# Reordering the turns of two 16-head attentions: a projection between first and second scores, the products behind them in the projection's bank, and VectorE's spare work bound behind the addition of maxima

## The chip, the cores and the metric

The kernel runs on one NeuronCore of a Trainium2 chip, as one program. The metric is the device time of one execution in microseconds (us). A NeuronCore has five engines that take their own instructions in the order in which the program lists them and wait for one another through semaphores: TensorE (PE; its weight loads are listed as PEld), VectorE (DVE), ScalarE (ACT), GpSimd (POOL) and SyncE (SP, which here only issues DMAs). Matrix products go to PSUM, which is cut into banks; SBUF is the on-chip memory, HBM the main one.

## The reference, cut to what matters

The model is a decoder of two layers on 8 batches of 256 tokens of 256 channels, all in float32. Each layer is a mixer, a cross attention and a last block, with a residual sum and a layer norm behind each:

```python
x = layernorm(x + L0_attn(x))    # a gated convolution
x = layernorm(x + L0_xattn(x))   # cross attention with 77 keys
x = layernorm(x + L0_ffn(x))     # shared and routed experts
x = layernorm(x + L1_attn(x))    # 16-head self attention with rotary embedding
x = layernorm(x + L1_xattn(x))   # cross attention
x = layernorm(x + L1_ffn(x))     # 16-head self attention with split masks
```

Only the fourth and the sixth matter here. Both project x to queries, keys and values of 16 heads of 16 channels and compute `softmax(q k^T * scale) v`, then an output projection and a bias. The fourth (called the first attention below) turns queries and keys by the rotary tables. The sixth (the second attention) splits the tokens into "positive" and "negative" ones by a similarity to a guide vector; each token attends only to its own class and to five register tokens, and the register tokens take the mean of both classes.

## The kernel before

The program runs the six blocks one after another; blocks overlap a little at their seams. Everything that the change touches is in the class `Heads16`, which both attentions use (`Rotary` for the first, `split` for the second), and in the list of extra work that `split` hands to it.

**A turn.** An attention has 8 batches, and a batch 4 groups of 4 heads, so `Heads16.run` makes 32 turns and two more to empty the pipeline. In turn i the loop issues:

- `scores(i)` (matmuls L1032): first scores, queries by keys, into two double banks of the pool tag `sc`. VectorE then takes the negated row maxima with two reductions (L1038).
- `products(i - 2)` (L1080): probabilities by values, into the single bank `op`. ScalarE copies the result to `o` (L1087), and in all batches but the last SP copies the rows with the sums of the softmax out into a compact tile `comp` (L1093).
- `exponentials(i - 1)` (L1061): second scores, keys by shifted queries, so that they come out transposed and with the maximum subtracted, into two more double banks of `sc`; ScalarE takes two exponentials from them into `pT` (L1069).
- the extra work of place 0: TensorE work in the bank `op`, such as transposes of finished tokens (L89), the register tokens' scores (L1535), the transposes of their probabilities (L1559) and their products (L1569).
- the extra work of place 1: a projection of a later batch (L1005 queries and keys, L1014 values) or the output projection of an earlier one (L1127), in the single bank `mm`, which ScalarE or VectorE empties.
- `turn_maxima(i)` (L1048): two transposes of the maxima into `op`; VectorE adds them to the queries, which gives the shifted queries `qs` (L1207 in the first attention, L1434 in the second).
- the extra work of place 2, mostly VectorE's: the reciprocals of the sums (L1100; SP writes them back as `rows`, L1102), the spreading and application of them (`wide` L1111, `o` L1119, `oT` L1122), the rotation of a later batch's queries and keys (`sw` L1226, then GpSimd L1230 to L1237), the statistics of a finished batch's layer norm (L111, L112), which GpSimd completes (L114, L115, L117), and the register tokens' softmax (L1546, L1553, then GpSimd L1554).

The `sc` pool has three double banks and a turn takes four, in rotation. So the second half of the second scores goes into the bank that the first half of the same turn's first scores had, and it has to wait for the first reduction.

**Whose order counts.** The framework puts instructions on each engine's queue by its own estimate of when they can run; `tc.issue_after(x)` holds everything issued inside it behind x on x's own engine. `bound(f)` holds TensorE's instructions of f behind TensorE's newest one, so TensorE's order is that of the code. All other work of a turn is held behind the turn's second reduction on VectorE, and what follows the second scores also behind the last exponential on ScalarE.

**The extra work by turns.** For batch b and t = 4b the first attention lists: the projections of queries and keys of batch b+1 in turns t+1 and t, their rotation one turn later, its values in t+3, the reciprocals in t+4 and t+6, `normed` (L1111 to L1122) in t+5 and t+7, the output projection in t+10 (t+8 for the last two batches), the layer norm (`finish`) in the turn after that, and the transposes of the finished tokens (`turn_out`, L89) in the second turn after it. The second attention lists the register tokens' four steps in t, t+1, t+2 and t+3, the same reciprocals, `normed`, output and `finish`, and the projections of batches 5 to 7, in turns given by hand in `at_turn`; batches 0 to 4 are projected ahead of the loop.

## Time and profile before

| | |
|---|---|
| median of 3 runs | 1399.26 us (1399.0 to 1399.41) |
| the profiled execution | 1399.1 us, of which its span on the core is 1397.3 us |
| busy share of the span | PE 96%, PEld 66%, DVE 57%, ACT 36%, POOL 30% |
| first attention | its turn 0 starts at 710.35 us, turn 31 at 888.32 us |
| second attention | its turn 0 starts at 1188.30 us, turn 31 at 1362.95 us; the span ends at 1397.3 us |

A page of the profile gives shares of the whole span, but the change touches two stretches of it, so those have to be read by themselves. The timeline lists start, length, engine, line, operation and tiles of each instruction or run of like ones, and in square brackets how long the engine sat idle before it and who ended that. "Granted clock" (PEclk) is the share of TensorE's full speed in a stretch.

The length of a turn is read from one first-score matmul to the next. In the middle of the first attention four turns take 6.06, 5.66, 5.67 and 5.67 us (turns 20 to 23 start at 827.18, 833.24, 838.91 and 844.57 us, turn 24 at 850.24); in the middle of the second, 5.13, 5.66, 5.84 and 6.56 us (turns 16 to 19 start at 1278.96, 1284.10, 1289.76 and 1295.60 us, turn 20 at 1302.16).

### The profile page before, as it was taken

Reading aid. Unit: us, or ns where it says so; the run is one execution under the profiler, and the core shown is the slowest. Engines: PE = TensorE matmul, PEld = TensorE weight load, DVE = VectorE, ACT = ScalarE, POOL = GpSimd, SP = SyncE. Lnnn points to the kernel's source line nnn. Section 1 sums busy time; section 2 is a strip of 40 time slices with the busy share of each in tenths; the row PEclk is TensorE's granted clock in tenths of the full one; section 3 lists DMA queues with packets and bytes.
Section 4 is the critical chain, followed back from the end, with each engine's and each line's share of the span. In section 5 each row is a group of like instructions: output and inputs, shape, how many; then the busy total and the mean of one; then the engine's idle time right before and its main releaser. Section 6 shows DMA issues by size and latency. Waiting matters only on the chain.

```text
span 1397.3 us, 21759 instructions
## 1 busy us (share of the span) xinstructions
PE 1335.6 (96%) x8521; PEld 928.5 (66%) x8521; DVE 793.6 (57%) x1514; ACT 496.5 (36%) x738; POOL 420.7 (30%) x467
## 2 busy tenths in 40 slices
PE   8999999999999999999989999899999998899994
PEld 3554578888876666656566666577878887566652
DVE  3776555565643423323656777755556662677774
ACT  3455532333331123221215444343332323344441
POOL 0100012223200123326423757332343545123322
PEclk9999999999999999999999999999999999899997
DMA  9000043334340012332130000025232210000000
GB/s 284 2 1 0 0 149 111 85 96 154 125 196 0 23 57 87 88 124 83 30 106 3 4 2 3 2 84 165 79 98 61 62 37 2 24 9 29 16 19 23
DMA packets 79113, 88.16 MB, mean 63 GB/s; under 512 B 13476, under 2 KB 73796, under 8 KB 78500
## 3 DMA queue, kind: packets, MB, share of 16 engines
q1 hardware_dynamic: 75604, 77.46, 17.7%
q0 software_dynamic: 3408, 9.31, 2.4%
q8 instruction: 68, 1.11, 0.3%
q14 instruction: 33, 0.27, 0.1%
HBM read 56.77 MB, written 29.52 MB: 62 GB/s over the span
## 4 chain that ended last, share of the span: by engine, by line
PE 71%; DVE 6%; POOL 3%; issue 2%; DMA 2%; SPq 0%; ACT 0%; POOLq 0%; DVEq 0%; ACTq 0%
PE mm L521 9%; PE sc L476 8%; PE mm L778 7%; PE ps_sc L1061 6%; PE ps_sc L1032 5%; PE mm L841 5%; PE op L1080 4%; PE tr L795 4%; PE ps_mm L1005 2%; PE tr L855 2%; PE ps_mm L1127 2%; PE sc L505 2%; PE sc L375 2%; PE sc L411 2%; PE sc L457 1%
## 5 line engine op out<-in xcount | busy, mean ns | idle before, releaser
L1038 DVE TENSOR_REDUCE mx<-ps_sc 128x4 f32<-128x1024 f32 x128 | 150.9, 1221 | 41.0 <-PE ps_sc L1032 40.9
L521 PE MATMUL mm<-Ub,pT 128*128 128x256 f32 (+1 forms) x640 | 144.6, 379 | 0.5 <-ACT pT L75 0.4
L496 POOL TENSOR_TENSOR p<-p,sm 128x616 f32<-128x616 f32 x60 | 72.7, 1216 | 240.1 <-DVE sm L493 213.5
L1069 ACT ACTIVATE pT<-ps_sc 128x1024 f32<-128x1024 f32 x128 | 124.1, 1021 | 56.6 <-PE ps_sc L1061 56.6
L476 PE MATMUL sc<-M,xT_s 128*128 128x308 f32 x512 | 139.0, 423 | 1.1 <-ACT pT L75 1.1
L521 PEld LDWEIGHTS mm<-Ub,pT 128*128 128x128 f32 (+1 forms) x640 | 120.8, 190 | 20.0 <-ACT pT L75 0.9
L476 PEld LDWEIGHTS sc<-M,xT_s 128*128 128x128 f32 x512 | 94.4, 188 | 35.3 <-ACT pT L75 2.1
L778 PE MATMUL mm<-xT_s,w 128*128 128x512 f32 x256 | 113.4, 595 | 2.1 <-DVE h L784 2.1
L489 ACT ACTIVATE p<-p 128x616 f32<-128x616 f32 x64 | 45.9, 716 | 154.6 <-DVE p L485 132.8
L1061 PE MATMUL ps_sc<-qs,kp 32*128 32x256 f32 x1024 | 99.4, 417 | 0.9 <-DVE mx L1038 0.9
L1061 PEld LDWEIGHTS ps_sc<-qs,kp 32*128 32x128 f32 x1024 | 64.9, 192 | 35.9 <-issue 26.6
L778 PEld LDWEIGHTS mm<-xT_s,w 128*128 128x128 f32 x256 | 47.8, 190 | 56.0 <-issue 52.6
L815 POOL DMA_INDIRECT xb<-xd,token x39 | 37.1, 952 | 146.4 <-PE tr L822 81.2
L483 DVE TENSOR_REDUCE nmx<-sc 128x8 f32<-128x616 f32 x64 | 51.1, 799 | 46.4 <-PE sc L476 46.3
L1080 PE MATMUL op<-pT,va 128*32 128x256 f32 x1024 | 71.3, 398 | 4.6 <-DVE qs L1207 4.0
L841 PE MATMUL mm<-wE,xbT 128*128 x156 | 73.5, 593 | 0.3 <-ACT xbT L827 0.3
L1087 ACT COPY o<-op 128x256 f32<-128x256 f32 x64 | 23.8, 373 | 131.8 <-PE op L1080 131.8
L492 DVE TENSOR_REDUCE sm<-p 128x8 f32<-128x616 f32 x64 | 50.6, 790 | 22.2 <-ACT p L489 21.8
L114 POOL TENSOR_SCALAR rstd<-mv 128x2 f32<-128x2 f32 x48 | 12.3, 255 | 166.9 <-DVE mv L112 166.8
L117 DVE TENSOR_SCALAR x_s<-r,mv,rstd 128x256 f32<-128x256 f32 x66 | 26.0, 436 | 60.9 <-POOL rstd L115 60.9
L827 DVE COPY hT<-tr 128x256 f32<-128x256 f32 x39 | 16.6, 425 | 75.7 <-PE tr L822 75.7
L181 PE MATMUL pair<-xT_s,w 128*128 128x512 f32 x128 | 58.3, 615 | 0.9 <-DMA w<-in_W_inT 0.9
(307 smaller groups left out, 2490.4 us busy)
## 6 DMA issues: line engine op xcount, KB each, us to landing
Ub<-ud SPq DMA_DIRECT2D x32, 512.0 KB
ud<-U SPq DMA_DIRECT2D x16, 616.0 KB
wE<-in_wE SPq DMA_DIRECT2D x4, 1536.0 KB
yd<-y SPq DMA_DIRECT2D x39, 128.0 KB
Ub<-ud SPq DMA_DIRECT2D x32, 104.0 KB
ud<-U SPq DMA_DIRECT2D x4, 608.0 KB
x_s<-in_x SPq DMA_DIRECT2D x8, 256.0 KB
w<-in_Wo SPq DMA_DIRECT2D x2, 1024.0 KB
```

Of the source, the lines that this page charges most:

```text
L181: last = nc.tensor.matmul(ps[:, i, :], w_in[:, kc, c * P : (c + 1) * P], xT_s[:, kc, :], start=kc == 0, stop=kc == 1,)
L476: nc.tensor.matmul(sc[:, a, : 4 * NCTX], xT_b[:, kc, j * P : (j + 1) * P], M[:, a * 4 : a * 4 + 4, kc, at : at + NCTX], start=kc == 0, sto ...
L496: engine.tensor_tensor(pv, pv, bcast(sm, 2, [P, 8, NCTX]), ALU.mult)
L521: nc.tensor.matmul(o[:, j * D : (j + 1) * D], pT[:n, c, j * P : (j + 1) * P],  Us[b][:n, g, c], start=g == 0 and j == 0 and c == 0, stop=g ...
L778: nc.tensor.matmul(ps, w[:, kc, cols], xT_s[:, kc, :], start=kc == 0, stop=kc == 1)
L795: nc.tensor.matmul(o[:, j * D : (j + 1) * D], hs[c][:, at : at + P], w3[:, c, :], start=c == 0, stop=c == 7,)
L841: nc.tensor.matmul(ps, xT[:, kc, :], column(j, kc * 512, 512), start=kc == 0, stop=kc == 1)
L1032: nc.tensor.matmul(scs[s // 2][:, s % 2, qb * SEQ : (qb + 1) * SEQ], self.queries(b, c, s, m)[:, qb * P : (qb + 1) * P], self.keys(b, c, s ...
L1038: self.last = nc.vector.tensor_reduce(self.mx[m][:, :, 2 * j : 2 * j + 2, self.free[m]].rearrange("p q s -> p s q"), scs[j].rearrange("p s ...
L1061: nc.tensor.matmul(scs[s // 2][:, s % 2, kb * SEQ : (kb + 1) * SEQ], self.keys(b, c, s, m)[:, kb * P : (kb + 1) * P], qs[s * 32 : (s + 1) ...
L1069: last = nc.scalar.activation(pT[:, 2 * j : 2 * j + 2].rearrange("p s k t -> p s (k t)"), scs[j], AF.Exp)
L1080: nc.tensor.matmul(ps[s * 32 : (s + 1) * 32, :SEQ], va[:, kb, 8 * c + 2 * s + m, :], pT[:, s, kb, :], start=kb == 0, stop=kb == 1, tile_po ...
```

## The change

Within a turn the order on TensorE becomes: first scores, place 0, place 1, second scores, products, transposes of the maxima. This holds where a turn has work of place 1 as well as products and second scores; then the products' copy on ScalarE stands between the two exponentials. In a turn without work of place 1 the products stay ahead of the second scores, but place 0 is still moved ahead of both. The products go to the bank `mm` in place of `op`. Work of place 2 is held behind `shifted`, the addition that makes `qs`, on VectorE. In the second attention the projections move to other turns, and `fill(0)` in the part ahead of the loop stands two steps later in the code.

```diff
-        def exponentials(self, i):
+        def exponentials(self, i, between):
...
-            for j in range(2):
-                last = nc.scalar.activation(
+            def exp(j):
+                return nc.scalar.activation(
                     pT[:, 2 * j : 2 * j + 2].rearrange("p s k t -> p s (k t)"), scs[j], AF.Exp
                 )
-            return last
+
+            first = exp(0)
+            with tc.issue_after(first.ins), tc.issue_after(self.newest(PE)):
+                copied = between()
+            with tc.issue_after((copied or first).ins):
+                return exp(1)
...
-            va, pT, ps = self.vals[b % 2], self.pT.pop(i), self.side()
+            va, pT, ps = self.vals[b % 2], self.pT.pop(i), self.mm()
...
                 with tc.issue_after(self.last.ins), ExitStack() as st:
-                    if 0 <= i - 2 < n:
+                    for f in work.pop((i, 0), ()):
+                        bound(f, self.side())
+                    other, products = work.pop((i, 1), ()), 0 <= i - 2 < n
+                    for f, end in other:
+                        ps = self.mm()
+                        bound(f, ps)
+                        end(ps)
+                    late = products and other and i - 1 < n
+                    if products and not late:
                         bound(self.products, i - 2)
                     if 0 <= i - 1 < n:
-                        st.enter_context(tc.issue_after(bound(self.exponentials, i - 1).ins))
-                    for f in work.pop((i, 0), ()):
-                        bound(f, self.side())
-                    ends = []
-                    for f, end in work.pop((i, 1), ()):
-                        ps = self.mm()
-                        bound(f, ps)
-                        ends.append(lambda end=end, ps=ps: end(ps))
+                        bound(
+                            self.exponentials, i - 1,
+                            lambda: self.products(i - 2) if late else None,
+                        )
                     if i < n:
-                        bound(self.turn_maxima, i)
-                    for f in ends + work.pop((i, 2), []):
+                        st.enter_context(tc.issue_after(bound(self.turn_maxima, i).ins))
+                    for f in work.pop((i, 2), []):
                         f()
...
-            at_turn = ((5, 9, 13), (11, 15, 17), (19, 21, 23))
+            at_turn = ((7, 8, 11), (12, 15, 16), (19, 20, 23))
...
             for i in range(3):
                 early(0, i)
-            fill(0)
             turn_last(at.mm())
             early(1, 0)
             add_last(at.mm())
+            fill(0)
```

`turn_maxima` and both `shifted` now return the addition's instruction, and `products` its copy, so that the loop can hold other work behind them.

More of the change, by code (lines that the diff above doesn't have):

```diff
@@ L948, in experts @@
         ]
+    PE = mybir.EngineType.PE
     class Heads16:
@@ L1052, in turn_maxima @@
             qs = self.qs[i] = self.c2.tile([P, SEQ], F32, tag="qs", name="qs")
-            self.shifted(b, c, m, qs, ps[:, :SEQ])
-        def exponentials(self, i):
+            return self.shifted(b, c, m, qs, ps[:, :SEQ])
+        def exponentials(self, i, between):
             b, k = divmod(i, 4)
@@ L1086, in products @@
             o = self.o[b, c]
-            nc.scalar.copy(o[:, m], ps[:, :SEQ])
+            copied = nc.scalar.copy(o[:, m], ps[:, :SEQ])
             if b == NB - 1:
-                return
+                return copied
             if m == 0:
@@ L1096, in products @@
             )
+            return copied
         def inverted(self, b, c):
@@ L1144, in run @@
             n = 4 * NB
-            pe = mybir.EngineType.PE
             def bound(f, *args):
-                with tc.issue_after(self.newest(pe)):
+                with tc.issue_after(self.newest(PE)):
                     return f(*args)
@@ L1206, in shifted @@
         def shifted(self, b, c, m, dst, maxima):
-            nc.vector.scalar_tensor_tensor(
+            return nc.vector.scalar_tensor_tensor(
                 dst, self.qrs[b % 2][:, c, :], self.cs["meets"][:, m : m + 1], maxima,
@@ L1433, in shifted @@
             def shifted(b, c, m, dst, maxima):
-                nc.vector.tensor_tensor(dst, qms[b][:, m, c, :], maxima, ALU.add)
+                return nc.vector.tensor_tensor(dst, qms[b][:, m, c, :], maxima, ALU.add)
             at = Heads16(st, queries, keys, shifted)
```

## The prediction

> **What bounds the kernel now.** I read the page's busy times, then its chain, then the two attentions alone by stretches and by timeline, since a share of the whole span averages six blocks.

> ```profile
> PE 1335.6 (96%) x8521; PEld 928.5 (66%) x8521; DVE 793.6 (57%) x1514; ACT 496.5 (36%) x738; POOL 420.7 (30%) x467
> ...
> PE 71%; DVE 6%; POOL 3%; issue 2%; DMA 2%; SPq 0%; ACT 0%; POOLq 0%; DVEq 0%; ACTq 0%
> ```

> The first line is busy time, the second the chain that ended last. TensorE sets the time nearly alone, so a change can win only where TensorE is busy without need, and loses wherever TensorE is made to wait. Busy by stretch (start:end, length, PE, PEld, DVE, ACT, POOL, PEclk, DMA share, GB/s), for turns 16 to 19 of the first attention and for its end:

> ```profile
> 804.10:827.20 23.10, 23.10 (x240) 15.95 (x239) 17.20 (x32) 11.04 (x16) 14.66 (x16) 1.00 0.02 3
> 892.10:905.00 12.90, 8.86 (x64) 5.37 (x65) 7.03 (x20) 3.94 (x6) 3.98 (x5) 0.74 0.01 1
> ```

> In a steady turn TensorE never stops; behind a stop of 4.04 us (892.41 to 896.45) its granted clock is halved for 6.83 us. Turns 19 and 20, by timeline:

> ```profile
> 821.51 1.15 PE L1032 MATMUL ps_sc<-kp,qr 32*128 32x256 f32 x16
> ...
> 822.63 1.07 PE L1080 MATMUL op<-pT,va 128*32 128x256 f32 x16
> 822.69 2.36 DVE L1038 TENSOR_REDUCE mx<-ps_sc 128x4 f32<-128x1024 f32 x2 [0.21 <-PE ps_sc L1032]
> ...
> 823.63 1.48 PE L1061 MATMUL ps_sc<-qs,kp 32*128 32x256 f32 x16
> ...
> 824.97 0.75 DVE L111 BATCH_NORM_STATS2 st<-r 128x6 f32<-128x256 f32 x2
> 825.04 1.99 PE L1014 MATMUL ps_mm<-w,xT_s 128*128 128x256 f32 x8
> ...
> 826.32 0.30 POOL L114 TENSOR_SCALAR rstd<-mv 128x2 f32<-128x2 f32 x1 [0.59 <-DVE mv L112]
> ...
> 826.70 0.89 POOL L115 TENSOR_TENSOR rstd<-rstd,nhalf 128x2 f32<-128x2 f32 x1
> 826.87 0.38 PE L1048 MATMUL op<-ident,mx 128*128 128x128 f32 x2
> ...
> 827.29 0.48 DVE L1207 SCALAR_TENSOR_TENSOR qs<-qr,cst,op 128x256 f32<-128x256 f32 x1 [0.27 <-PE op L1048]
> 827.70 2.43 POOL L117 TENSOR_SCALAR x_s<-r,mv,rstd 128x256 f32<-128x256 f32 x2
> ...
> 830.71 0.66 PE L89 MATMUL op<-ident,x_s 128*128 128x128 f32 x4
> ```

> Two things to see. The second scores take 1.48 where they take 1.09 in turns in which the first reduction is done already: 0.36 us of every turn is a wait, the gain that is to be had. And the layer norm of a batch starts at 824.97, 1.90 ahead of the maxima's transposes (T, 826.87), and ends at 830.13, 5.16 later; L89 reads it at 830.71. The margin is 0.58 us. In the second attention the register tokens' probabilities have the same shape:

> ```profile
> 1288.22 0.16 DVE L1553 RECIPROCAL nsm<-nsm 128x1 f32<-128x1 f32 x1
> ...
> 1288.48 0.66 POOL L1554 TENSOR_SCALAR nsl<-nsl,nsm 128x256 f32<-128x256 f32 x1 [1.75 <-DVE nsm L1553]
> ...
> 1289.45 0.38 PE L1048 MATMUL op<-ident,mx 128*128 128x128 f32 x2
> ...
> 1293.29 0.44 PE L1559 MATMUL op<-ident,nsl 128*128 128x128 f32 x2
> ```

> They are ready 0.31 before T and are read 3.8 after it.

> **The change, part by part.** All times are counted from T, the start of a turn's L1048.

> *1. Projection ahead of the second scores.* A turn is then first scores 1.08, projection 1.83, second scores 1.09, products 1.00, T 0.34: 5.34. The projection hides the 0.36. One more change of matmul shape costs an unknown amount: nothing at best; the step from first scores to products, with a change, shows 0.1 at most, so bounds 0 to 0.2; I take 0.1. So 5.43 against 5.67, **-0.24**, in 12 turns of the first attention: -2.9. Turns 1 to 5, where the projections are many, give -1.6 by the same sum (0.36 less, where it is there).

> *2. Place 2 bound behind qs.* Now this work starts 0.45 + 0.48 = 0.93 after T instead of before T, so it stands ahead of the next turn's two reductions (2.36). `wide`, `o`, `sw`, `oT` take 1.72 together. So the reductions end at 0.93 + 1.72 + 2.36 = 5.0. In turns 10, 14, ... 30 the output projection is then emptied by VectorE's sum with `xb` (0.69), which stands behind the reductions: 5.7. The products now need that bank (part 4): with 0.15 of handing over, 1.0 of products, T comes at 6.85 instead of 5.67: **+1.2** in 6 turns, +7.2. Bounds: +0.2 (if only the second scores waited) to +1.4. Turn 6, which has no projection to cover, goes from 4.02 to about 4.97: +0.95. Reciprocals with or without `sw` (0.24, 0.91) fit in the 5.43.

> *3. Place 0 moved to right behind the first scores.* This is the dear one. The layer norm (L111) now starts at T + 0.93 - 0.1, and takes 5.16 plus 0.35 for the `va` copies (0.74, ahead of rstd on POOL by the changed order, half of it beside VectorE's part): done at T + 6.3. TensorE reaches L89 at T + 0.34 + 1.08 = T + 1.4. **It waits 4.9** (bounds 4.4, with the first half of x_s 1.22 earlier and little else late, and 5.2). Behind it in TensorE's queue stand the projection, the second scores, the products and T; ScalarE's exponentials and VectorE's qs wait for these. Turns 12, 16, 20, 24: 6.3 + 0.4 (rest of L89) + 1.92 + 1.09 + 1.0 = 10.7 against 6.06, +4.7 each, +18.8. Turn 28, which had 5.33, has 8.9: +3.6. At the end, L89 of the sixth batch, behind turn 31, stands in the same way: +3 (0 to 5).

> Sum of the first attention: -1.6 - 2.9 + 7.2 + 0.95 + 18.8 + 3.6 + 3 = **+29.0**.

> *The second attention.* Here place 0 has the transposes L1559 behind POOL's `nsl`. Its chain starts behind qs: T + 0.87, and 1.58 from `wide` to `nsl` (1287.56 to 1289.14): ready at T + 2.4, asked for at T + 1.4: **+1.0** in 8 turns, those of remainder 2. The projections moved by `at_turn` go from turns of remainder 1 (5.67, then 3.98) into those of remainder 0 (5.13, then 6.73, since 2.65 of VectorE's work stands ahead of the reductions); remainder 3 goes from 6.56 to 6.37. By groups: turns 1 to 5 -3.6, 6 and 7 +0.6, 8 to 11 +0.1, 12 to 23 +1.9, 24 to 27 0, 28 to 30 +1.2. The `rows` DMAs stand behind the outputs and `kp` loads on SP's queue; a spreading that waits for them now holds back the reductions too: up to 6, I take +2.9; tail +1. Sum **+4.1** (-4 to +12).

> *4. Products in the bank `mm`, and ScalarE's copy between the exponentials.* The projection's copy (0.59) has the second scores' 1.09 to hide in; the products' copy (0.37) has the first scores' 1.08. The second exponential comes 1.4 later, and is next needed by products a turn on, 4 us away. Nothing, except where VectorE empties the bank (part 2). The move of `fill(0)` changes no order on VectorE or POOL: nothing; ±1 bounds it.

> *5. The clock.* Five waits (turns 12 to 28) are longer than any steady one. Stops of 2.15 and 2.19 (676.6, 160.6) leave PEclk at 1.00; one of 2.38 (714.65) and one of 4.04 halve it for 6.83. A wait of 3.7 for the first half of x_s and 0.9 for the second should halve it. Behind it L89 takes 0.91 against 0.49, a projection 2.5 against 1.83, second scores 2.02 against 1.09: +2.0 each, **+10** (0 to 17).

> [...]

> **Sum.** 1399.1 + 29.0 + 4.1 + 10 = 1442.2. The profiled execution (span 1397.3 and 1.8 around it) is 0.16 below the median of 1399.26. I say **1442**.

> **Rivals.**

> *The clock holds.* Two stops here left it at 1.00. Then 1432. Against it: 4.04 and 2.38 did not.

> *VectorE becomes the bound.* Everything late on VectorE delays its reductions, these T, and T the place 2 work; if SP's rows (6 instead of 2.9) and the clock (17) take their upper ends, and split +5 more, 1442 + 3 + 7 + 5 = 1457. For it: VectorE has 17.20 of 23.10 already. Against it: in most turns TensorE's own 5.43 is longer.

> *On the other side: place 2 leaves the path.* If VectorE ran this work in idle time ahead of T (it has 5.9 idle of 23.10), the reductions would start as now, so part 2 costs nothing; and if x_s were complete by T + 1.4, thus the layer norm 4.9 earlier, L89 would not wait and the clock would not fall. Then parts 1 and 3 leave -1.6 - 2.9 in the first attention and, with `nsl` 1.0 earlier, -4 in the second: **1391**. It decides on where L111 comes to run: it pays from 4.9 earlier on, and at today's 1.9 ahead of T (3.26 after T done) would still wait 1.9. The changed order has L111 behind qs, which speaks against it.

> *It does nothing on balance:* the wait of 0.36 stays, because another operand of the second scores is late, and part 3 is hidden by something I overlook: 1399.

> **How the numbers follow.** The forecast, 1442 with its bounds 1432 to 1452: 0.68. Clock holds, 1432 and a little below: 0.12. VectorE, 1457: 0.12. Covered waits, 1391: 0.05. Nothing: 0.03. The range must leave out at most 2 in 10: it runs from the low ends (clock 0, split -4 and stalls 4.4: 1442.2 - 10 - 8 - 2.5, about 1422, less 2 for the +0.2 of part 2 in some turns: 1420) to the third case, 1458. A measurement of this kernel can tell 0.2%, 2.8 us, from no change. Faster 0.05, same 0.03, slower 0.92.

> **What would show it.** Turns of the first attention by their first scores: 10.7, 5.4, 6.8, 5.4 in place of 6.06, 5.66, 5.67, 5.67; at their head L89 idle 3.7 and 0.9 behind POOL's x_s, and PEclk at half behind it; second scores at 1.09 in late turns (part 1); products idle behind VectorE's r in turns 10 to 30 (part 2); L1559's successor in the second attention idle 1.0 behind `nsl`. If L89 starts without a wait, or turns of remainder 0 take under 7 us, the prediction is wrong at its largest term.

## The result and the profile after

The changed kernel takes **1443.76 us** (median of 4 runs, 1443.15 to 1444.23) against 1399.13 us (4 runs, 1398.86 to 1399.41): a ratio of **1.0319**, with a 95% interval of 1.0301 to 1.0337. The profiled execution has a span of 1442.4 us, 45.1 more than before. The forecast was 1442, with a range of 1420 to 1458.

Busy time by engine, and the chain that ended last, on the page of the changed kernel:

```profile
PE 1352.7 (94%) x8521; PEld 928.5 (64%) x8521; DVE 786.9 (55%) x1514; ACT 495.4 (34%) x738; POOL 420.5 (29%) x467
...
PE 66%; DVE 8%; POOL 5%; issue 3%; DMA 2%; ACT 1%; SPq 1%; POOLq 0%; DVEq 0%; ACTq 0%
```

Lines are numbered by each run's own kernel: L1032, L1048, L1061, L1080, L1207 and L1559 of the kernel before are L1034, L1050, L1064, L1088, L1219 and L1571 here.

The same 8521 matmul records take 17 us longer, though none was added: the mean granted clock fell from 0.983 to 0.969. TensorE's share of the chain falls by 5 points, and VectorE and GpSimd take 4 of them: TensorE waits for them. Where, the starts of the turns tell. The table gives times between first scores, in the last row from turn 31 of the second attention to the end of the span:

| stretch | before | after | difference |
|---|---|---|---|
| up to turn 0 of the first attention | 710.35 | 710.73 | +0.4 |
| first attention, turns 0 to 12 | 70.72 | 73.23 | +2.5 |
| turns 12 to 28 | 92.23 | 120.20 | **+28.0** |
| turns 28 to 31 | 15.02 | 22.42 | +7.4 |
| turn 31 to the second attention | 299.98 | 301.71 | +1.7 |
| second attention, turns 0 to 31 | 174.66 | 178.36 | +3.7 |
| to the end | 34.37 | 35.76 | +1.4 |

The first attention holds 37.9 of the 45.1 us. By stretches (length, busy PE, PEld, DVE, ACT, POOL, PEclk, DMA share, GB/s), the changed kernel's turns 16 to 19 and then the time right behind the wait in turn 20:

```profile
813.35:843.30 29.95, 25.34 (x236) 16.25 (x236) 16.87 (x33) 10.88 (x16) 14.61 (x16) 0.89 0.01 2
846.90:853.75 6.85, 5.87 (x24) 4.25 (x28) 1.25 (x2) 0.58 (x1) 1.40 (x2) 0.50 0.00 0
```

The same four turns took 23.10 with TensorE always busy; now 4.6 of 29.95 are idle, and the clock is at half behind the long wait (0.50 in the second row). Turns 19 and 20 of the changed kernel, by timeline:

```profile
840.64 1.28 POOL L1243 TENSOR_TENSOR sw<-sw,rot 128x512 f32<-128x512 f32 x1
...
842.00 1.27 POOL L1245 TENSOR_TENSOR qr<-qk,sw 128x512 f32<-128x512 f32 x1
842.27 0.20 PEld L1050 LDWEIGHTS op<-ident,mx 128*128 128x128 f32 x2 [0.41 <-issue]
842.27 0.44 PE L1050 MATMUL op<-ident,mx 128*128 128x128 f32 x2
...
842.75 0.48 DVE L1219 SCALAR_TENSOR_TENSOR qs<-qr,cst,op 128x256 f32<-128x256 f32 x1 [1.91 <-PE op L1050]
...
843.14 0.74 DVE L111 BATCH_NORM_STATS2 st<-r 128x6 f32<-128x256 f32 x2
843.22 0.73 POOL L1025 COPY va<-vn 128x256 f32<-128x256 f32 x2
...
843.32 1.15 PE L1034 MATMUL ps_sc<-kp,qr 32*128 32x256 f32 x16 [0.61 <-POOL qr L1245]
...
844.50 0.30 POOL L114 TENSOR_SCALAR rstd<-mv 128x2 f32<-128x2 f32 x1 [0.55 <-DVE mv L112]
...
845.87 2.43 POOL L117 TENSOR_SCALAR x_s<-r,mv,rstd 128x256 f32<-128x256 f32 x2
...
847.15 0.47 PE L89 MATMUL op<-ident,x_s 128*128 128x128 f32 x1 [2.68 <-POOL x_s L117]
...
848.35 0.90 PE L89 MATMUL op<-ident,x_s 128*128 128x128 f32 x3 [0.73 <-POOL x_s L117]
...
849.05 3.62 PE L1007 MATMUL ps_mm<-xT_s,w 128*128 128x256 f32 x8
```

L111 now starts 0.87 after T (842.27), where it started 1.90 ahead of it. L89 asks behind the first scores, finds neither half of x_s, and is idle 2.68 and 0.73. The projection behind it takes 3.62 where it takes 1.99 undisturbed. And a wait that the prediction did not have: the first scores themselves stand 0.61 for `qr`, since the rotation (`sw`, then four steps on GpSimd) also starts behind qs.

What TensorE waited for between 710 and 927 us, by the waits of the changed kernel (total, times, longest):

```profile
PE op L89 <- POOL x_s L117: 17.6, 10, 2.8
PE ps_sc L1034 <- POOL qr L1245: 3.5, 6, 0.6
PE ps_mm L1088 <- DVE r L104: 3.1, 5, 0.7
```

And in turn 14 of the second attention (timeline), where the register tokens' probabilities come late:

```profile
1308.97 0.15 DVE L1565 RECIPROCAL nsm<-nsm 128x1 f32<-128x1 f32 x1
...
1309.22 0.65 POOL L1566 TENSOR_SCALAR nsl<-nsl,nsm 128x256 f32<-128x256 f32 x1 [3.83 <-DVE nsm L1565]
...
1309.93 0.44 PE L1571 MATMUL op<-ident,nsl 128*128 128x128 f32 x2 [1.63 <-POOL nsl L1566]
```

They were ready ahead of T; now TensorE stands 1.63 us for them here, 4.7 in six turns together.

### The profile page after: what moved, and what is told of

Its sections match the earlier page's. It is cut to its first block, busy times and chain, and to the rows that moved or that the text cites. A ratio compares the mean times of both kernels' runs of the same rounds, so it can differ in the third digit from the quotient of the medians.

```text
span 1442.4 us, 21723 instructions
## 1 busy us (share of the span) xinstructions
PE 1352.7 (94%) x8521; PEld 928.5 (64%) x8521; DVE 786.9 (55%) x1514; ACT 495.4 (34%) x738; POOL 420.5 (29%) x467
## 4 chain that ended last, share of the span: by engine, by line
PE 66%; DVE 8%; POOL 5%; issue 3%; DMA 2%; ACT 1%; SPq 1%; POOLq 0%; DVEq 0%; ACTq 0%
PE mm L521 8%; PE sc L476 8%; PE mm L778 8%; PE mm L841 5%; PE ps_mm L1088 4%; PE tr L795 4%; PE ps_sc L1064 4%; PE ps_sc L1034 3%; PE ps_mm L1007 3%; PE tr L855 2%; PE sc L505 2%; DVE mx L1040 2%; PE sc L375 2%; PE ps_mm L1136 2%; PE sc L411 2%
## 5 line engine op out<-in xcount | busy, mean ns | idle before, releaser
L1072 ACT ACTIVATE pT<-ps_sc 128x1024 f32<-128x1024 f32 x128 | 128.9, 1025 | 102.4 <-PE ps_sc L1064 102.4
L521 PEld LDWEIGHTS mm<-Ub,pT 128*128 128x128 f32 (+1 forms) x640 | 121.0, 190 | 19.7 <-ACT pT L75 0.9
L778 PE MATMUL mm<-xT_s,w 128*128 128x512 f32 x256 | 115.1, 603 | 2.1 <-DVE h L784 2.1
L1064 PE MATMUL ps_sc<-qs,kp 32*128 32x256 f32 x1024 | 85.5, 417 | 1.8 <-DVE mx L1040 1.8
L778 PEld LDWEIGHTS mm<-xT_s,w 128*128 128x128 f32 x256 | 48.5, 193 | 57.0 <-issue 53.9
L1088 PE MATMUL ps_mm<-pT,va 128*32 128x256 f32 x1024 | 71.8, 394 | 6.7 <-DVE r L104 3.1
L1064 PEld LDWEIGHTS ps_sc<-qs,kp 32*128 32x128 f32 x1024 | 54.3, 194 | 31.7 <-issue 23.8
L114 POOL TENSOR_SCALAR rstd<-mv 128x2 f32<-128x2 f32 x48 | 11.7, 243 | 177.4 <-DVE mv L112 177.3
L117 DVE TENSOR_SCALAR x_s<-r,mv,rstd 128x256 f32<-128x256 f32 x66 | 26.0, 436 | 60.9 <-POOL rstd L115 60.9
L254 PE MATMUL pair<-xc,w 128*128 128x512 f32 x128 | 58.6, 601 | 0.0
L1386 POOL TENSOR_TENSOR ssq<-ssq,nhalf 128x32 f32<-128x32 f32 x8 | 43.4, 5430 | 51.3 <-DVE ssq L1383 51.3
```

Source lines behind the costliest of these rows:

```text
L254: last = nc.tensor.matmul(ps[:, i, :], w_dt[:, kc, c * P : (c + 1) * P], xc[s][kc // 2][:, kc % 2, :], start=kc == 0, stop=kc == 3,)
L521: nc.tensor.matmul(o[:, j * D : (j + 1) * D], pT[:n, c, j * P : (j + 1) * P],  Us[b][:n, g, c], start=g == 0 and j == 0 and c == 0, stop=g ...
L778: nc.tensor.matmul(ps, w[:, kc, cols], xT_s[:, kc, :], start=kc == 0, stop=kc == 1)
L1064: nc.tensor.matmul(scs[s // 2][:, s % 2, kb * SEQ : (kb + 1) * SEQ], self.keys(b, c, s, m)[:, kb * P : (kb + 1) * P], qs[s * 32 : (s + 1) ...
L1072: return nc.scalar.activation(pT[:, 2 * j : 2 * j + 2].rearrange("p s k t -> p s (k t)"), scs[j], AF.Exp)
L1088: nc.tensor.matmul(ps[s * 32 : (s + 1) * 32, :SEQ], va[:, kb, 8 * c + 2 * s + m, :], pT[:, s, kb, :], start=kb == 0, stop=kb == 1, tile_po ...
```

## The experiments

They ran on two chips, e8, e10 and e11 on one, the others on the other. Executions of one kernel spread there over some 10 us (before: 1390.49 to 1400.92), so a verdict rests on the ratio with its interval, and the reading on the stages of one profiled execution of each run. Below, the remainder of a turn is that of its number by four, and a late turn is one with the products behind the second scores.

| run | turns 12 to 28 | first attention | second attention | span |
|---|---|---|---|---|
| before | 92.23 | 177.97 | 174.66 | 1397.3 |
| changed | 120.20 | 215.85 | 178.36 | 1442.4 |
| e1: place 2 free | 103.73 | 191.10 | 186.68 | 1421.0 |
| e2: place 0 late | 99.96 | 188.30 | 178.47 | 1412.8 |
| e3: both | 93.05 | 175.99 | 182.70 | 1400.7 |
| e4: wait filled | 113.13 | 204.01 | 176.96 | 1431.0 |
| e5: second attention bound | 93.06 | 177.65 | 180.66 | 1399.2 |
| e6: and old turns | 93.06 | 177.69 | 187.40 | 1406.7 |
| e7: products in `op` | 123.58 | 224.02 | 211.58 | 1486.0 |
| e8: L89 a turn later | 95.95 | 183.11 | 180.31 | 1409.1 |
| e9: emptying first | 89.92 | 173.88 | 186.76 | 1403.9 |
| e10: first attention only | 89.92 | 173.81 | 173.45 | 1386.0 |
| e11: emptying first in both | 89.92 | 173.84 | 185.22 | 1399.1 |

One profile each leaves room for chance, because the clock falls in other turns from profile to profile (e5 at 1325.93 to 1332.75, for one, below). The second attention is the same code in the changed kernel, e4 and e8, and takes 178.36, 176.96 and 180.31; so are the first attentions of e3, e5 and e6, with 175.99, 177.65 and 177.69, where the difference stands in turn 1. So differences of up to 3.4 in the second attention and 1.7 in the first tell nothing by themselves.

### Which edit makes the wait: e1, e2, e3

My theory was that the long wait needs both edits: the binding that makes the layer norm late, and the move that makes L89 early. The rivals gave the loss to one of them. Place 2 free again (e1):

```diff
-                        st.enter_context(tc.issue_after(bound(self.turn_maxima, i).ins))
+                        bound(self.turn_maxima, i)
```

> The changed kernel with place 2 no longer held behind qs; projection first, place 0 right behind the first scores and the products' bank stay. My theory: the long wait needs both edits, a layer norm that starts 2.8 us later and an L89 that asks 3 us earlier. With the layer norm back where it was (1.9 ahead of T, done at T + 3.26), L89 asked for at T + 1.4 waits 0.65 and 0.7 in turns 12 to 28 and the clock holds; the sum r of the output projection still keeps the products waiting about 1 us in turns 10, 14, ... 30. 1404 (1398 to 1410). Rival A (place 0's move alone makes the loss): 1430 or more. Rival B (the binding alone makes it): 1400 or less.

Measured: 1.016 (1.013 to 1.0189), median 1420.8. TensorE's wait for x_s between 700 and 960 us (total, times, longest; 17.6 in the changed kernel):

```profile
PE op L89 <- POOL x_s L117: 8.8, 10, 0.9
```

The mechanism is as expected, L89 idle 0.95 and 0.8 in turns 12 to 28; the size isn't. 8 us come from the second attention (186.7, changed kernel 178.4; turns 17 and 25 take 9.06 and 10.11 in place of 3.96), and two of the four turns are slow behind their stops all the same (turns 16 and 24 take 9.5, turns 12 and 20 7.9; in turn 16 the projection takes 2.74 and the second scores 1.93, where they take 1.99 and 1.08 undisturbed).

Place 0 back behind the second scores (e2, `zero()` runs the work of place 0):

```diff
-                    for f in work.pop((i, 0), ()):
-                        bound(f, self.side())
...
-                            lambda: self.products(i - 2) if late else None,
+                            lambda: (zero(), bound(self.products, i - 2))[1] if late else None,
                         )
+                    zero()
```

> The changed kernel with place 0 back behind the second scores (between them and the products, or behind them where the products stand ahead); the binding behind qs stays. My theory: L89 asks at T + 4.4 and x_s is there in halves at T + 4.9 and 6.0, so 1.2 us of wait is left and the clock holds; the register tokens' transposes no longer wait: 1443.8 less 22 and 8, so 1412 (1405 to 1420). What is left over the kernel before is VectorE's place 2 ahead of the reductions. Rival A (place 0's move alone): 1400 or less. Rival B (the binding alone): 1436 or more.

Measured: 1.0171 (1.0139 to 1.0203), median 1420.56, just above the expected range; the profiled execution took 1414.54, with a span of 1412.8. The clock stays at 1.00 in the first attention up to the end of turn 28 (888.6), and L89 waits 0.6 at most:

```profile
PE op L89 <- POOL x_s L117: 2.9, 5, 0.6
```

Both edits undone (e3):

> The changed kernel with both undone: place 2 free, place 0 behind the second scores. Left are the projection ahead of the second scores, the products in the projection's bank, and the projections' turns in the second attention. My theory: late turns at 5.43 in place of 5.67, L89 without a wait, but about 1 us in turns 10, 14, ... 30 where r stands behind reciprocals and sw: 1397 (1392 to 1401). Rival (products in the projection's bank or the change of matmul shapes cost more than the 0.36 gained): 1402 or more.

Measured: 1.004 (1.0023 to 1.0057), median 1402.82, in the rival's range. The second attention is slower than before by 8, which I had not expected. The first seems faster (175.99 against 177.97), but that is turn 1 (5.88 against 8.63), most of which the kernel before ran at half clock (718.28 to 725.11). From turn 2 to turn 31 it takes 163.09 against 162.32, because products still wait for VectorE's r:

```profile
PE ps_mm L1088 <- DVE r L104: 3.3, 4, 0.8
```

What follows, for the first attention: neither edit 176.0; the binding alone 188.3 (+12.3); place 0 alone 191.1 (+15.1); both 215.9 (+39.9). **12.5 us are the product of the two**, in neither by itself; 10.9 of them stand behind turn 1, the rest in turns 0 and 1 (time from turn 2 to turn 31: 163.1, 175.4, 177.7 and 200.9). Both rivals fall.

### What the clock costs: e4

```diff
             def turn_out(b, ps):
                 s, half = divmod(b, 2)
+                w = self.W[2]
+                for _ in range(10 if b < 5 else 0):
+                    nc.tensor.matmul(ps[:, :D], w[:, 0, :P], w[:, 0, :], start=True, stop=True)
                 transposed(
```

> The changed kernel with ten needless matmuls (128 by 256, 0.23 us each at full clock, into the bank that L89 then overwrites) ahead of L89 in turns 12, 16, 20, 24 and 28, so that TensorE is busy for 2.3 of the 2.7 us of the first wait. If the halved clock behind that wait is a cost of its own, PEclk stays at 1.00, L89, projection and second scores come back to 0.5, 1.9 and 1.1, and each of the five turns loses 2 to 2.5 us: 1432 (1429 to 1435). Rival (the slow records behind the wait cost nothing more, or the fill delays x_s): 1443 or more.

Measured: 1.0279 (1.0249 to 1.0308), median 1435.67. Turn 20 by stretch, in the run with the filled wait:

```profile
841.25:851.45 10.20, 10.17 (x82) 7.69 (x82) 4.83 (x11) 2.17 (x4) 4.29 (x6) 1.00 0.00 0
```

Busy throughout, at full clock, and shorter: 10.20 in place of 12.25, though the fill (each of the ten is two records, 4.42 us in all where 2.3 were expected) is longer than the wait needs. From turn 12 to turn 31 it saves 142.62 - 132.28 = 10.3. Without the halved clock, the time from the end of the first scores to the projection would be 2.68 + 1.2 until the second half + 0.35 for the rest of L89 (0.70 at half clock) = 4.23; the fill makes it 4.42 + 0.44 = 4.86, 0.6 too long, five times 3.1. So the halved clock costs some **13 us** in these turns, an estimate from these rows; 10.3 of it is measured as saved.

### Only the asking, moved: e8

```diff
-                put(o + 2, 0, lambda ps: turn_out(b, ps))
+                put(o + 3, 0, lambda ps: turn_out(b, ps))
```

> The changed kernel with the finished tokens' transposes (L89) one turn later in the first attention, all else as changed. Theory: x_s is done 6.0 after T of the turn before; a turn on, L89 asks some 7 after it and waits no more, so the clock holds too. Turns of remainder 0 come to about 6.0, those of remainder 1 to 6.0 (with L89): turns 12 to 28 take 99 in place of 120, the whole some 24 less than the changed kernel: ratio to before 1.012 to 1.018. Rival (the binding by itself delays these turns, whoever waits): 1.025 or more.

Measured: 1.0076 (1.0052 to 1.0099), median 1408.61: more than expected. L89 no longer waits, turns 16 to 19 take 5.50, 5.84, 6.50 and 6.12, and the mean granted clock of the run is 0.984, where the changed kernel's is 0.969. One number in one line gives back 33 us of the span, 32.7 of it in the first attention. Against e3, which has neither edit, what is left of the binding there is 0.16 in turn 18 and 0.67 in turn 19 (the next first scores behind `qr`). Turn 18 has a further 0.78 (6.34 in e3, 5.56 in e9), the products' wait for r, which is there without the binding too.

### The products' bank: e7

```diff
-            va, pT, ps = self.vals[b % 2], self.pT.pop(i), self.mm()
+            va, pT, ps = self.vals[b % 2], self.pT.pop(i), self.side()
```

> The changed kernel with the products in the bank op, as before, all else as changed. Theory: the products then no longer wait for r in turns 10 to 30, but the maxima's transposes, right behind them and in the same bank, wait in every late turn until ScalarE has copied the products out (0.37 and some 0.2 of handing over): late turns 6.0 in place of 5.45, some 30 of them, so slower than the changed kernel by 8 to 16 us, ratio to before 1.038 to 1.044. Rival (the products' bank is of no weight): 1.032; a gain, if the wait for r weighs more: under 1.03.

Measured: 1.0642 (1.0613 to 1.0671), median 1487.12. The timeline of the run with products in `op`, turn 13:

```profile
805.55 1.07 PE L1088 MATMUL op<-pT,va 128*32 128x256 f32 x16
...
807.11 0.44 PE L1050 MATMUL op<-ident,mx 128*128 128x128 f32 x2 [0.49 <-ACT o L1095]
```

The transposes wait 0.49 for the copy, 40 times, 19.7 us: late turns are 6.01, as expected. The loss, 43 us, is nearly three times the upper end of what I expected. Products also queue behind the results of place 0 in that bank: they wait 20.5 us in all until VectorE has emptied it, most of it in turns without place 1, and above all in the last turns of the second attention (53.5 where the changed kernel takes 37.5 from turn 24 on). Late products pay only with the move to `mm`.

### The second attention: e5, e6, e11

Place 2 held behind qs there alone (e5; an attribute `hold` tells the two attentions apart):

```diff
-                        st.enter_context(tc.issue_after(bound(self.turn_maxima, i).ins))
+                        shifted = bound(self.turn_maxima, i)
+                        if self.hold:
+                            st.enter_context(tc.issue_after(shifted.ins))
```

> The changed kernel with place 0 behind the second scores in both attentions, and place 2 held behind qs in the second attention alone. In the run with both undone the first attention took 176.0 us from its turn 0 to its turn 31 (before: 178.0), the second 182.7 (before: 174.7); with only place 0 undone the second took 178.5. Theory: the binding costs in the first attention (its layer norm is read two turns on) and pays in the second, where unbound reciprocals that wait for the compact sums stand ahead of what the next turn needs. So 176.0 and 178.5: about 4 us less than with both undone, ratio to before 0.998 to 1.001. Rival (the second attention's 182.7 comes from the projections' new turns alone): no change against both undone, ratio 1.004.

Measured: 1.0035 (1.002 to 1.0049), median 1401.99, second attention 180.66. Not told apart from e3's 1.004: by the stages some of it is as expected (turns 12 to 24 take 72.52 in place of 75.56), and turns 24 to 31 give it back (42.05 in place of 40.15). There turns 24 and 25 ran in part at half clock (1325.93 to 1332.75); e2, whose second attention is the same code, took 39.52 there and 178.47 in all. The time is inconclusive.

The projections in the turns of the kernel before (e6, `at_turn` as before, else as e5):

> As the run with the second attention alone bound, and its projections in the turns of the kernel before. Theory: a projection in a turn of remainder 0 (7.05 with it, 5.1 without) costs more there than in one of remainder 1 (3.96 without, 5.45 with), by 0.4 to 0.6 in each group of four turns where it was moved: second attention 176.5 in place of 178.5, ratio to before 0.996 to 0.999. Rival (it doesn't matter which turn has it): as the run before it.

Measured: 1.0078 (1.0055 to 1.0101), median 1408.22. **This theory fell**, by sign. With the old turns, a turn of remainder 0 has no projection, VectorE's place 2 stands ahead of the reductions, and the second scores take 3.0 where they take 1.08 undisturbed. So such a turn takes 6.72, hardly less than the 7.05 with a projection in it, and turns 16 to 19 together 24.61 in place of 23.75. Of the 6.7 us between the two runs, 2.9 stand in one turn (21, 8.33 where turns 13 and 17 take 5.44); the mean granted clock is 0.984 in e5 and 0.981 in e6. The moved projections are the cover for the binding.

So I expected the old turns to be good without the binding (e11: as e9 below, with `hold = False` for both):

> As the run with VectorE's emptying first, and the second attention the same way: place 2 not held behind qs but behind the emptying, its projections in the turns of the kernel before. Theory: the binding was what made the old turns dear (second scores of 3.0 in turns of remainder 0, where no projection covers the reductions); without it they come back to 1.45 and the second attention to 172 to 176, ratio to before 0.993 to 0.999. Rival (reciprocals that wait for the compact sums still stand ahead of the next turn's needs): second attention 180 or more, ratio 1.001 or more.

Measured: 1.003 (1.0017 to 1.0043), median 1401.21, second attention 185.22. **This fell too**, to its rival. Timeline of the run, turn 12 of the second attention:

```profile
1253.15 0.25 DVE L1110 RECIPROCAL comp<-comp 128x16 f32<-128x16 f32 x1 [2.76 <-DMA comp<-o]
1253.32 0.36 DVE L1562 TENSOR_TENSOR nsl<-op,hidden 128x256 f32<-128x256 f32 x1
...
1253.73 0.44 PE L1051 MATMUL op<-ident,mx 128*128 128x128 f32 x2 [2.71 <-DVE nsl L1562]
```

VectorE stands 2.76 for the compact sums; behind that reciprocal is `nsl`, which empties the bank that T needs. Products at the end of a turn send their sums later than products at its head, and the reciprocal that reads them has kept its place. In the kernel before the same reciprocal (at 1259.20) follows the reductions without a wait. Over the second attention VectorE's waits for these sums, all in runs where place 2 is not held behind qs there, are 8.1 us in e1, 9.4 in e11, and in e3:

```profile
DVE comp L1109 <- DMA comp<-o: 9.3, 4, 2.4
```

Neither the kernel before nor the changed one has such a line, nor have e2 and e5: before, the products stood early; with the binding behind qs the reciprocal comes late as well. That is what the binding buys in the second attention.

### The version that is faster than both: e9, e10

In the first attention r was late too, behind reciprocals and `sw`. Place 2 is held behind VectorE's newest instruction once the projection's bank is emptied (e9, old turns as in e6):

```diff
+                    emptied = self.newest(mybir.EngineType.DVE)
                     late = products and other and i - 1 < n
...
+                        else:
+                            st.enter_context(tc.issue_after(emptied))
```

> As the run with the projections' old turns, and in the first attention place 2 held behind VectorE's emptying of the projection's bank, so that r stands ahead of reciprocals and sw. Theory: turns 10, 14, ... 30 go from 6.34 to 5.6, six times 0.7, 4 us less than the run without it: ratio to before 0.993 to 0.997, faster than both kernels. Rival (place 2 that starts later is late for the next turn's reductions): no gain.

Measured: 1.0044 (1.0022 to 1.0066), median 1404.04. In the first attention as expected: turns 14, 18, 22 and 26 go from 6.34 to 5.56, the attention to 173.88. The whole is not faster, since it carries the second attention of e6. With the second attention's loop and turns as in the kernel before (e10):

```diff
+                if self.hold:
+                    with tc.issue_after(self.last.ins), ExitStack() as st:
+                        if 0 <= i - 2 < n:
+                            bound(self.products, i - 2)
...
+                    continue
```

> The first attention as in the run with VectorE's emptying first (projection ahead, place 0 behind the second scores, place 2 free but behind r), the second attention as in the kernel before. Theory: 173.9 us in the first attention in place of 178.0, the second at 174.7 again: 4 us less than the kernel before, ratio 0.995 to 0.999. Rival (the gain is given back at the seam to the block behind): 1.000 or more.

Measured: **0.9942** (0.992 to 0.9965), median 1389.58 against 1397.43 of the kernel before on that chip. Turns 16 to 19 of this run by stretch:

```profile
801.05:823.55 22.50, 22.46 (x239) 14.43 (x238) 17.33 (x33) 10.97 (x16) 14.73 (x16) 1.00 0.02 2
```

22.5 in place of 23.1, with TensorE as busy as before. The attention gains 4.2: 3.1 from turn 2 to turn 31, and 1.1 in turn 1, most of which the kernel before spent at half clock. More than expected comes from behind it: turn 31 to the second attention takes 293.99 in place of 299.98, since the wait of 4.04 there is now one of 1.14 and some shorter ones, and the mean granted clock from 884 to 1178 us is 0.99 in place of 0.98. All runs with place 0 late and place 2 not held behind qs in the first attention show the shorter time there (e3, e5, e6, e9, e10, e11: 294.0 to 295.4).

## Why the prediction was right

- **Part 1, right.** Turns with the projection ahead take 5.45 for the predicted 5.43, where nothing else waits. With r ahead (e10), turns 12 to 28 gain 2.3 of the predicted 2.9. Turns 1 to 5 did not give their 1.6: only turns 4 and 5 gain (0.22 each), apart from turn 1, where the half clock lies at 717.18 to 724.01 in place of 718.28 to 725.11.
- **Part 2, the wait is there, its cause was wrong in the main, and one wait was missing.** Products wait for r, VectorE's sum that empties the output projection's bank, in turns 10 to 26: turn 18 takes 6.51 for the predicted 6.85, +0.84 in place of +1.2. The prediction put this down to the binding behind qs; but without it (e3) turn 18 still takes 6.34, and 5.56 once r is moved ahead of reciprocals and `sw` (e9). So 0.17 is the binding's, and 0.78 comes of r's place in VectorE's order, now that the products need r's bank. The binding does cost turn 6 its 0.9 (4.94; 3.96 in e3). What I did not see is `qr`: the rotation is place 2 as well, so the first scores of turns 8, 12, ... 28 wait up to 0.6, and turns of remainder 3 take 6.12 for the predicted 5.43.
- **Part 3, right in kind, the wait too long.** Predicted 4.9 per turn, measured 3.4 (2.68 and 0.73). x_s is done 6.03 after T for the predicted 6.3: the `va` copies cost nothing, they ran at 843.22, before rstd could start. And TensorE asks 2.2 after T for the predicted 1.4, mostly because of the wait for `qr` (0.61). Turn 28 took 10.38 for the predicted 8.9 and 2.0 of clock.
- **Part 5, too small.** Predicted 10, some 13 by e4. I had charged L89, a projection and second scores at the same 2.0 each time; in turn 28 the products, the second scores and the next turn's first scores also run at half clock (1.87, 2.02, and 2.63 with a wait). No run shows the prediction's upper end of 17, nor the 7 that its second rival takes from it: e4 saved 10.3 and puts the cost at some 13, though the spells at half clock are as long in all as the prediction took them to be (34.1 us in turns 12 to 31). The prediction also went by the length of a stop alone; but one of 2.15 near 676.6 was followed by half clock in the changed kernel and by full clock in the kernel before (below).
- **Turns 12 to 28 together**: 4 x 6.7 + 4 x 1.2 - 8 x 0.24 = 29.7 predicted, 28.0 measured. Turns 20 to 23 take 12.25, 5.45, 6.51 and 6.12 for the predicted 12.7, 5.43, 6.85 and 5.43: 30.33 against 30.41. Errors of opposite sign (a shorter wait, an r that came earlier; a dearer clock, `qr`) let the sum come out better than its parts.
- **Turns 0 to 12**: -0.4 predicted, +2.5 measured. Early turns with L89 behind the first scores did not gain (turns 2 and 3 lose 0.45 and 0.58), and turns 7 and 11 wait for `qr`.
- **Second attention**: +3.1 predicted without the tail, +3.7 measured, but its parts were off, and that the sum agrees is luck: the same code takes 176.96 to 180.31 in three profiles. Turns 1 to 5 gained 2.1 in place of 3.6, turns 6 and 7 lost 1.9 for 0.6, and turns 12 to 23 lost 4.2 for 1.9. The 2.9 for SP's queue hardly shows: VectorE stood 1.8 us in all for `rows`, 1.3 before. The 1.0 for `nsl` came: first scores to L1571 take 1.0 to 2.1 longer in turns 6, 10, ... 30. That the binding and the moved projections pay for each other there (e6) was not in the prediction at all.

Of the rivals, the clock that holds and VectorE as the bound did not come about. The rival on the other side named its deciding point as the place where L111 comes to run, and said that L89 would still wait 1.9 with L111 at its old place, 1.9 ahead of T; in e1 L111 runs 1.62 ahead of T, and L89 waits 0.95 and 0.8.

Open: how much of the 8 us that the second attention loses in e3 belongs to the reciprocals that wait for the sums (9.3 us on VectorE, not all of it TensorE's), how much to the moved projections, and how much to where the clock falls; e5 and e11 do not separate them. Why the clock falls behind an interval idle for 0.37 of its length and not behind another idle for 0.50 (both in the kernel before, below) is open too.

## What to carry to other kernels

When an operand is made later by one edit and its reader earlier by another, price the pair: in the first attention here each alone cost 12 and 15 us, both cost 40. Before work is moved ahead on the bounding engine, find for each instruction of it how long its operand has been ready; a margin of 0.58 us does not survive a move by three. And an edit that looks like a detour of its own (projections put elsewhere) may be the cover for another edit, so that undoing it alone says little about it (e6).

## What the runs showed of the hardware

Cut into intervals of 3.41 us on that grid, from the first record of the clock on (11.72 and 10.62), the two profiles have 17 intervals at full clock in which TensorE was idle for 0.63 to 1.00 of the length, and half clock followed each of them. It followed none of the 757 idle for 0.31 or less. Nine lie between: half clock followed three (idle 0.37 at 1342.92 and 0.57 at 1158.60 in the kernel before, 0.47 at 928.81 in the changed one) and full clock six, among them one idle 0.50 (at 1155.19 in the kernel before) and one idle 0.57 (at 160.81 in the changed one). This is a count over two profiles, and where between 0.31 and 0.63 the clock falls it does not show.

Nor did the length of a stop alone tell. A stop of 2.15 near 676.6 was followed by 1.00 in the kernel before, where it lies across two intervals (TensorE busy 2.70 and 1.98 of 3.41), and by 0.50 from 679.64 to 683.05 in the changed kernel, where it lies within one (busy 1.27); the eight matmuls L778 behind it took 3.70 and 5.40. A stop of 2.19 at 160.6 left the clock at 1.00 in the kernel before, where it lies across two intervals, and was followed by 0.50 in e1, where it lies within one. Two intervals of each, first the kernel before, then e1 (length, busy PE, PEld, DVE, ACT, POOL, PEclk, DMA share, GB/s):

```profile
158.49:161.91 3.42, 2.13 (x11) 1.13 (x9) 3.35 (x5) 2.08 (x2) 0.00 (x0) 1.00 0.00 0
161.91:165.32 3.41, 2.51 (x18) 2.35 (x20) 1.86 (x3) 2.34 (x2) 0.00 (x0) 1.00 0.02 5
...
160.12:163.53 3.41, 1.22 (x11) 0.98 (x9) 2.54 (x4) 3.35 (x4) 0.00 (x0) 1.00 0.00 0
163.53:166.94 3.41, 3.41 (x17) 3.10 (x17) 2.63 (x3) 0.67 (x1) 0.00 (x0) 0.50 0.02 5
```

And in e1's turn 16 two stops of 0.89 and 0.87, from 808.69 to 810.78, lie within one interval of its grid: behind them come the projection of 2.74 and the second scores of 1.93.
